# Dealing edge items by TensorE time in a sparse graph network, and writing its tables from ScalarE's queue

## The chip, the core and the metric

The kernel runs on one core of a Trainium2 chip. A core has a matrix engine (TensorE, "PE" in the profile, its weight loads "PEld"), VectorE ("DVE"), ScalarE ("ACT"), GpSimd ("POOL") and a fifth engine that only issues DMAs (SyncE, "SP"). Each engine works through its own queue in order and waits on semaphores for the others; a "q" behind an engine's name (SPq, ACTq) is the queue of that engine, where DMA issues and semaphore waits stand. The metric is device microseconds of one execution.

## The reference

Thirty-two samples of a graph of N = 512 nodes with D = 256 features pass through four layers that share one adjacency matrix `adj` (512 x 512, about 1.8% of its cells nonzero).

```python
def gnn(h, adj, W1, b1, W2, b2, Wa, ba, Wm, bm, beta1, beta2, beta3):   # layers 0 and 3
    pre_u = einsum('bud,dk->buk', h, W1[:D]); pre_v = einsum('bvd,dk->bvk', h, W1[D:])
    hidden = relu(pre_u[:, :, None, :] + pre_v[:, None, :, :] + b1)
    S = sigmoid(einsum('buvk,ko->buvo', hidden, W2)[..., 0] + b2[0])
    a = einsum('buv,bud->bvd', S * adj, h)
    m = einsum('uv,bud->bvd', adj, h) * h
    return beta1 * h + beta2 * (a @ Wa + ba) + beta3 * (m @ Wm + bm)

def layer1(z):  return z + relu(einsum('ij,bjd->bid', adj, z) @ W.T + b)

def layer2(x):
    feats = x @ W1.T
    f1 = feats @ W2 + b2[0]
    coefs = softmax(leaky_relu(f1[:, :, None] + f1[:, None, :]) + adj, axis=-1)
    return coefs @ feats + bias2 + x
```

The gate S is wanted only where `adj` is not zero, since it is multiplied by it.

## The kernel before

**Tiling.** The samples are worked in 8 groups of NB = 4 samples. A sample's 512 nodes lie in NC = 4 chunks of 128 partitions, its 256 features in DC = 2 chunks. A branch at run time takes a path for sparse adjacencies (class `Sparse`); it is the one that runs here, and everything below is of it.

**The edges.** For each group and each of the layers 0 and 3, `pre` (lines 662 to 687) multiplies the turned features by W1: for each sample b and chunk c TensorE's two matmuls (L672, L674) give both halves, VectorE adds the bias to one half while it copies it to the tile `puv` (L677), ScalarE copies the other half (L680), VectorE sums a few mixed columns (L682), and a DMA (L686) writes `puv` (256 KB) to a table in device memory. `puv` has three buffers. The DMA of a piece isn't issued at once: `self.later` holds it, and `settle` issues it, on SP's queue, in the next piece or at the end of a stage.

When a group's table stands, `edges` (L715 on) runs 40 turns, the "edge items". For each of them GpSimd gathers rows of the table by an indirect DMA (L711; the fixed side `mine` is loaded on SP's queue, L766), VectorE takes the maximum, the minimum and a sign product (L805, L807, L806), the row is summed by VectorE (L825) or by ScalarE (L791), and after every few items a sigmoid follows (L749, ScalarE's exponential at L696, L700, L701, L755). The values are scattered by GpSimd (L705) into a dense array of cells, which `load` reads back as the tile `SA`.

**The middle stage.** `middle` and `middle_one` do the rest of layer 0, layers 1 and 2 and the tables of layer 3 for the four samples of a group, as a sequence of pieces (each `yield` ends one). For a sample b they are, in order: `mhT` (two pieces, L49 and VectorE's L874); `pz` (two, L964); `Wm` (two, L971, with VectorE adding to the tile hT, now zT, at L972); `zW` (two, L985, copied by ScalarE at L989); `yT` (two, L49 with `adjT` and zW, ScalarE's L995, VectorE's L996); `feats` (four, L1007, ScalarE's L1015); the softmax (f1 at L1023, and for each of four chunks ScalarE's L1031, VectorE's L1032 and L1034, ScalarE's exponential at L1035, VectorE's L1036 and the scaling L1037; `put_back` turns a finished chunk on TensorE at L1076 and ScalarE copies it at L1077); between the last put_backs the next sample's `hWa` (two, L49 with Wa); the weighted sum `pv` (two, L49 with eT, VectorE's L1054 making xT in the buffer of yT); `flat` for the next sample (ScalarE, L933); `pre` for layer 3 (four); and turning x2 back (two, L1065, ScalarE's copy L1067 and DMA L1068, issued on ScalarE's queue). For group 0, `hWa` and `mhT` have been made ahead (`middle_before`) and aren't in the stage. The last stage of a group (`last`: L49, L1125, L1134) and the first stage of a later one (`first`: turning the input, L658 and L659, then `pre`) are streams of their own.

**The order.** `weave` (L543 on) takes all streams, each with a list of times for its pieces, sorts all pieces by time, and has them emitted in that order. The times only order the pieces; they aren't times on the chip. The middle stages are the "main" streams. A stage's pieces get times in proportion to the shares that `middle_shares` lists: `spread` gives each piece its start, and the next piece starts as much later as the share says. The 40 turns of an edge stream lie at even steps over a stretch of time. So a piece with a large share has more edge items behind it in the queues. For group g's middle stage these are items of layer 0 of the next group and of layer 3 of the group before. Pieces of `first` and `last` ("fill") run only behind a middle piece that yields True (the last one of Wm, zW, yT, feats and pv, and each of the softmax): one of them, or two when four or more are due. The operations of an edge item are kept by `behind` from being scheduled ahead of the middle piece two back.

**Ends.** Before the first middle stage lies a prelude (the lists of edges, group 0's tables and edge items), behind the last one the layer 3 edges and the last stage of group 7.

Of the kernel before, what the change touches and what calls it, by code (L numbers as in the profile page):

```python
# [19 lines left out]
NC = N // P  # L20
DC = D // P
G = 32
NB = 4
# [28 lines left out]
class Model:  # L52


    def __init__(self, ctx, tc, a):
        nc = self.nc = tc.nc
        self.tc, self.a = tc, a
        const = self.const = ctx.enter_context(tc.tile_pool(name="const", bufs=1))

        self.cols = const.tile([P, 2, 2, DC, 1], F32, name="cols_W2_b1")  # L60
        for k, L in enumerate(("L0_gnn", "L3_gnn")):
            nc.gpsimd.dma_start(self.cols[:, k, 0], a[f"{L}_W2"].rearrange("(c p) o -> p c o", p=P))
            nc.gpsimd.dma_start(self.cols[:, k, 1], a[f"{L}_b1"].rearrange("(c p o) -> p c o", p=P, o=1))
        self.ident = const.tile([P, P], F32, name="ident")
        make_identity(nc, self.ident)
        self.adj = const.tile([P, NC, N], F32, name="adj")
        for c in range(NC):
            nc.sync.dma_start(self.adj[:, c, :], a["adj"][c * P : (c + 1) * P, :])
        self.g0, self.g3 = self.gnn_first("L0_gnn"), self.gnn_first("L3_gnn")
# [444 lines left out]
class Sparse:  # L514
# [3 lines left out]
    def __init__(self, ctx, m, counts, xr, outr, B):  # L518
        self.m, self.nc, self.tc, self.counts = m, m.nc, m.tc, counts
        tc = m.tc  # L520
        self.xr, self.outr = xr, outr
        pool = lambda n, b, **k: ctx.enter_context(tc.tile_pool(name=n, bufs=b, **k))
        self.dram = pool("dram", 1, space=bass.MemoryType.DRAM)

        self.cells = {
            k: [self.dram.tile([CELLS + SPARE, NB], F32, name=f"cells_{k}{q}") for q in range(2)] for k in "03"
        }
        self.lists = self.dram.tile([N, 2 * N], F32, name="lists")
        self.x2s = self.dram.tile([B, P, NC, D], F32, name="x2s")

        self.xT, self.x2T = (self.dram.tile([B, P, DC, N], F32, name=n) for n in ("xT", "x2T"))
        self.e = Edges(m, pool("edges", 1))
        self.adjT = pool("adjT1", 1).tile([P, NC, N], F32, name="adjT")
        self.grp = pool("grp", 2)
        self.act, self.small, self.gath = pool("act", 1), pool("small", 2), pool("gath", 6)
        self.ps = pool("ps", 7, space=PSUM)
        self.ps_f1 = pool("ps_f1", 1, space=PSUM)
        self.later, self.bigs, self.given, self.marks = None, 0, None, {}

    def psum(self):  # L540
        return self.ps.tile([P, N], F32, name="pst", tag="pst")
# [120 lines left out]
    def pre(self, g, b, hT):  # L662

        nc, w = self.nc, g.w
        rows = g.table.rearrange("(c p k) (b d) -> p c k b d", p=P, k=2, b=NB)
        for c in range(NC):
            cs = slice(c * P, (c + 1) * P)
            if c % 2 == 0:
                two = [self.psum() for _ in range(2)]
                for k, pp in enumerate(two):  # L670
                    ks = slice((c + k) * P, (c + k + 1) * P)
                    nc.tensor.matmul(pp, hT[:, 0, ks], w["W1"][:, 0::DC, :], start=True, stop=False)  # L672
            pp = two[c % 2]
            nc.tensor.matmul(pp, hT[:, 1, cs], w["W1"][:, 1::DC, :], start=False, stop=True)  # L674
            puv = self.small.tile([P, 2, D], F32, name="puv", bufs=3)
            part, mixed = (g.parts[:, k, c, b : b + 1] for k in range(2))
            nc.vector.scalar_tensor_tensor(  # L677
                puv[:, 0, :], pp[:, 0:D], 1.0, w["bu"], ALU.mult, ALU.add, accum_out=part
            )
            nc.scalar.copy(puv[:, 1, :], pp[:, D:])  # L680
            junk = self.small.tile([P, MIXED.stop - MIXED.start], F32, name="mixed", bufs=1)
            nc.vector.scalar_tensor_tensor(  # L682
                junk, puv[:, 0, MIXED], 1.0, w["sign"][:, 0, :], ALU.mult, ALU.mult, accum_out=mixed
            )
            self.settle()
            self.later = lambda c=c, puv=puv: nc.sync.dma_start(rows[:, c, :, b, :], puv)  # L686
            yield

    def settle(self):

        if self.later:
            self.later()
        self.later = None

    def exp_of(self, w, t):
        self.behind(self.nc.scalar.activation(t, t, AF.Exp, bias=w["nb2"], scale=-1.0))  # L696
# [18 lines left out]
    def edges(self, g, spare=()):  # L715
# [9 lines left out]
        mine = {}  # L725
        places = g.table.rearrange("(c p k) n -> c k p n", p=P, k=2)
        first, mixed, behind = (slice(0, MIXED.stop), MIXED, slice(MIXED.stop, D))
        sign = w["sign"][:, 1, :].unsqueeze(1).to_broadcast([P, NB, MIXED.stop - MIXED.start])

# [149 lines left out]
    def first(self, g, i):  # L879


        def load(b):
            h = self.act.tile([P, NC, D], F32, name="h0", tag="h", bufs=2)
            self.nc.sync.dma_start(h, self.xr[i + b])
            return h

        h = load(0)
        for b in range(NB):
            ahead = load(b + 1) if b < NB - 1 else None
            hT = self.turned(h, "hT0", "hT")  # L890
            yield
            self.nc.scalar.dma_start(self.xT[i + b], hT)
            yield from self.pre(g, b, hT)
            h = ahead
        self.settle()

    def middle_before(self, g0, i):

# [13 lines left out]
    def middle(self, g0, g3, i):  # L912


        SA = self.load(g0, 0)
        given, self.given = self.given, None
        h, hT = self.fresh(i, given)
        hT = hT()
        hWa = None
        if not given:  # L920
            for hWa in self.hWa(g0, hT, 0):
                yield
        flat = self.flat(SA, 0)
        for b in range(NB):
            keep = [h, hT, hWa, flat]
            yield from self.middle_one(g0, g3, b, i + b, SA, keep, given)
            h, hT, hWa, flat = keep
        self.settle()

    def flat(self, SA, b):  # L930
        flat = self.act.tile([P, NC, N], F32, name="flat", tag="eT")
# [255 lines left out]
def middle_shares(given):  # L1187


    hWa = [] if given else [1.7, 1.7]  # L1190
    shares = list(hWa)
    for b in range(NB):
        more = hWa if b < NB - 1 else []
        shares += [] if given else [2.8, 2.8]
        shares += [3.4, 3.4, 1.0, 2.7]
        shares += [1.7, 3.4, 2.8, 4.5] + [0.9] * NC
        shares += [0.4, 0.4, 0.4, 1.0, 0.4, 1.0] + more + [1.5, 1.5]
        shares += [2.8, 4.5] + [0.4] * NC + [0.5, 0.5]
    return shares + [0.1]


# [1 line left out]
def sparse_path(ctx, m, counts, xr, outr, B):  # L1203
# [10 lines left out]
    for t in range(last + 1):  # L1214
# [17 lines left out]
        if t == last:  # L1232
            end -= 0.2
            edges3 = edge_times(end + 0.003, end + 0.02, end + 0.45, end + 0.46, LEAD_AT_ENDS)
            behind = end + 0.29, end + 0.45
        streams += [
            (sp.first(g0, t * NB), first, "fill"),
            (sp.edges(g0, ("yT", "mhT3") if t == 0 else ()), edges0, ""),
            (sp.middle(g0, g3, t * NB), spread(middle_shares(t == 0), start, end), "main"),
            (sp.edges(g3, ("yT", "h1", "hT1") if t == last else ()), edges3, "free"),  # L1240
        ]
# [245 lines left out]
```

## Time and profile before

| | |
|---|---|
| median of 3 runs | 3185.09 us (3176.19, 3185.09, 3185.63) |
| profiled execution | 3185.67 us |
| its span in the profile | 3184.0 us |
| mean granted clock of TensorE | 0.936 |
| busy: PE, DVE, ACT, POOL | 2747.2, 2113.7, 1345.4, 1571.7 us |
| prelude and stage of group 0 | 0 to 264, 264 to 507 us |
| stages of groups 1 to 6 | 507 to 2690 us, about 364 us each |
| stage of group 7, end | 2690 to 2910, 2910 to 3184 us |

A row of the profile's groups names line, engine, operation, output <- input by the program's names, and the number of them; a DMA's row ends with the time from issue to landing. A row of the waits names who waited, for whom, the total in microseconds, how often, and the longest. Where zT is added in the tile hT, it is called hT; xT lies in the tile yT. In group 3 the four samples' stretches are 1230 to 1321, 1321 to 1407.7, 1407.7 to 1503 and 1503 to 1594 us. The granted clock is a share of TensorE's full speed.

### The profile page before, as it was taken

The page shows a single profiled execution, that of the slowest core. Times are in us where ns is not written, and L with a number is a line of the kernel's source. Part 1 is how long each engine was busy: PE and PEld are TensorE (multiplying, and loading weights), DVE is VectorE, ACT ScalarE, POOL GpSimd, SP SyncE. Part 2 cuts the span into 40 slices and gives each one's busy share as a digit, 9 for nine tenths or more (in the row PEclk, how much of TensorE's full clock was granted, in tenths as well). Part 3 has the DMA queues.
Part 4 walks back from the last instruction along what each step waited for, and adds up shares of the span by engine and source line. Part 5 has one row for each costly group of instructions (what it writes and reads, how often), then busy time and mean ns, then how long its engine had stood idle before and what let it go on. Part 6 is the DMA issues. An engine that isn't in the chain of part 4 may idle for free. (4 is left out here: it accounts for less than half of the span.)

```text
span 3184.0 us, 32606 instructions
## 1 busy us (share of the span) xinstructions
PE 2747.2 (86%) x8729; PEld 1664.7 (52%) x8730; DVE 2113.7 (66%) x5600; ACT 1345.4 (42%) x4185; POOL 1571.7 (49%) x1519
## 2 busy tenths in 40 slices
PE   6555888879998899989998899988999799989948
PEld 3333444445664565545654465545654466545637
DVE  6662686667587785777667785777758684773651
ACT  3343554444354343544345343544335343543330
POOL 2462454556455563555445563456535563450460
PEclk9787889999999999999999999999999999989979
DMA  8874557777678766887678766686678766651763
GB/s 282 288 228 152 187 188 228 241 261 221 207 236 261 238 220 220 264 263 227 200 242 265 260 222 213 228 283 217 202 236 263 267 217 219 197 188 66 244 199 113
DMA packets 315329, 712.73 MB, mean 224 GB/s; under 512 B 57600, under 2 KB 175360, under 8 KB 306944
## 3 DMA queue, kind: packets, MB, share of 16 engines
q0 software_dynamic: 133824, 439.85, 42.8%
q1 hardware_dynamic: 162928, 234.01, 22.5%
q10 hardware_dynamic: 18384, 36.71, 3.1%
q8 instruction: 71, 1.16, 0.2%
q14 instruction: 122, 1.00, 0.1%
HBM read 564.28 MB, written 146.15 MB: 223 GB/s over the span
## 5 line engine op out<-in xcount | busy, mean ns | idle before, releaser
L705 POOL DMA_INDIRECT cells<-s,cell x640 | 718.1, 1122 | 774.6 <-DMA cells<-s,cell 571.7
L711 POOL DMA_INDIRECT rows<-table,iv x556 | 598.4, 1076 | 612.1 <-DMA less<-less 235.5
L791 ACT ACTIVATE rows<-rows 128x256 f32<-128x256 f32 x1164 | 470.5, 406 | 620.8 <-DVE rows L807 371.4
L805 DVE TENSOR_TENSOR rows<-rows,mine 128x576 f32<-128x576 f32 x618 | 463.1, 749 | 238.8 <-DMA rows<-table,iv 215.9
L49 PE MATMUL pst<-adj,h 128*128 128x512 f32 x1024 | 452.2, 593 | 0.0
L825 DVE TENSOR_REDUCE s<-rows 128x4 f32<-128x1024 f32 x327 | 396.3, 1212 | 3.1
L49 PE MATMUL pst<-L_gnn_Wa,hT 128*128 128x256 f32 x1024 | 269.6, 415 | 131.8 <-DMA hT<-xT 73.2
L807 DVE TENSOR_TENSOR rows<-rows,mine 128x448 f32<-128x448 f32 x618 | 380.6, 616 | 0.0
L49 PEld LDWEIGHTS pst<-adj,h 128*128 128x128 f32 x1024 | 193.1, 191 | 220.4 <-issue 217.2
L49 PEld LDWEIGHTS pst<-L_gnn_Wa,hT 128*128 128x128 f32 x1024 | 210.6, 211 | 181.8 <-issue 68.0
L677 DVE SCALAR_TENSOR_TENSOR puv<-pst,L_gnn_bu 128x256 f32<-128x256 f32 x256 | 107.0, 418 | 238.5 <-DMA table<-puv 166.1
L49 PE MATMUL pst<-eT,feats 128*128 128x512 f32 x512 | 233.9, 611 | 12.9 <-ACT eT L1077 12.9
L49 PE MATMUL pst<-adjT,zW 128*128 128x512 f32 x512 | 226.3, 595 | 7.5 <-ACT zW L989 7.5
L985 PE MATMUL pst<-WT,hT 128*128 128x256 f32 x512 | 150.9, 460 | 79.6 <-DVE hT L972 79.6
L791 ACT ACTIVATION_READ_ACCUMULATOR rows<-rows 128x1 f32 x1164 | 219.3, 188 | 0.0
L1125 PEld LDWEIGHTS pst<-hWa,SA 128*128 128x128 f32 x896 | 213.7, 327 | 7.7 <-issue 5.0
L1125 PE MATMUL pst<-hWa,SA 128*128 128x256 f32 x896 | 216.8, 398 | 0.0
L933 ACT COPY flat<-SA 128x512 f32<-128x512 f32 x128 | 136.6, 1125 | 186.5 <-DMA SA<-cells 80.4
L680 ACT COPY puv<-pst 128x256 f32<-128x256 f32 x256 | 92.3, 370 | 249.1 <-DVE puv L677 246.2
L964 PE MATMUL pst<-flat,hWa 128*128 128x512 f32 x448 | 196.8, 592 | 0.0
L985 PEld LDWEIGHTS pst<-WT,hT 128*128 128x128 f32 x512 | 118.3, 236 | 118.9 <-DVE hT L972 54.4
L806 DVE TENSOR_TENSOR rows<-rows,L_gnn_sign 128x128 f32<-128x128 f32 x618 | 171.7, 279 | 0.0
(215 smaller groups left out, 4009.9 us busy)
## 6 DMA issues: line engine op xcount, KB each, us to landing
table<-puv SPq DMA_DIRECT2D x256, 256.0 KB, 5.1
SA<-cells POOLq DMA_DIRECT2D x64, 1024.0 KB, 6.2
h<-in_x_dram SPq DMA_DIRECT2D x64, 512.0 KB, 6.0
mine<-table SPq DMA_DIRECT2D x64, 512.0 KB, 6.7
rows<-table POOLq DMA_DIRECT2D x62, 512.0 KB, 6.3
hT<-xT SPq DMA_DIRECT2D x36, 512.0 KB, 5.1
h<-x2s SPq DMA_DIRECT2D x36, 512.0 KB, 4.9
xT<-hT ACTq DMA_DIRECT2D x32, 512.0 KB, 6.9
```

Of the source, the lines that this page charges most:

```text
L49: nc.tensor.matmul(out, lhsT, rhs, start=(n == 0), stop=(n == len(pairs) - 1))
L705: self.nc.gpsimd.indirect_dma_start(out=g.cells[half], out_offset=bass.IndirectOffsetOnAxis(ap=at, axis=0), in_=s, in_offset=None)
L711: self.nc.gpsimd.indirect_dma_start(out=rows, out_offset=None, in_=g.table, in_offset=bass.IndirectOffsetOnAxis(ap=at, axis=0))
L791: self.behind(nc.scalar.activation(part, part, AF.Identity, accum_out=g.s[:, k, b : b + 1]))
L805: self.behind(nc.vector.tensor_tensor(rows[:, :, first], rows[:, :, first], other[:, :, first], ALU.max))
L806: nc.vector.tensor_tensor(rows[:, :, mixed], rows[:, :, mixed], sign, ALU.mult)
L807: self.behind(nc.vector.tensor_tensor(rows[:, :, behind], rows[:, :, behind], other[:, :, behind], ALU.min))
L825: nc.vector.tensor_reduce(g.s[:, k, :], rows, AX.X, ALU.add)
L933: self.nc.scalar.copy(flat[:, r, :], SA[r][:, :, b])
L964: nc.tensor.matmul(pz, hWa[:, r, cs], flat[:, r, :], start=(r == 0), stop=False)
L985: nc.tensor.matmul(pw[:, at], zT[:, d, cs], m.WT_1[:, d, :], start=(d + k == 0), stop=(d * k == 1))
L1125: nc.tensor.matmul(pz[:, k * D : (k + 1) * D], SA[r][:, cs, b], hWa[:, r, :], start=(r + k == 0), stop=False)
```

## The change

Two things are changed. `middle_shares` gives other shares to the same pieces of the middle stage: a sample's sum (with hWa and mhT) goes from 52.0 to 71.2; the softmax's pieces go from 0.4 and 1.0 to 1.5 and 2.5, the pieces behind which fill runs grow by about 1, pre's go from 0.4 to 1.0. The number of pieces and the streams' stretches of time stay, so the stage as a whole has the same items; which of its pieces they stand behind is new. And the DMA that writes `puv` to the table is issued on ScalarE's queue in the piece itself, where it was held back by a piece and issued on SP's queue; `settle` and `later` go. All other instructions stay.

```diff
@@ pre @@
-            self.settle()
-            self.later = lambda c=c, puv=puv: nc.sync.dma_start(rows[:, c, :, b, :], puv)
-            yield
-
-    def settle(self):
-
-        if self.later:
-            self.later()
-        self.later = None
+            nc.scalar.dma_start(rows[:, c, :, b, :], puv)
+            yield
...
@@ first, middle @@
-        self.settle()
...
@@ middle_shares @@
     for b in range(NB):
-        more = hWa if b < NB - 1 else []
+        more = 0.0 if given or b == NB - 1 else 1.7
         shares += [] if given else [2.8, 2.8]
-        shares += [3.4, 3.4, 1.0, 2.7]
-        shares += [1.7, 3.4, 2.8, 4.5] + [0.9] * NC
-        shares += [0.4, 0.4, 0.4, 1.0, 0.4, 1.0] + more + [1.5, 1.5]
-        shares += [2.8, 4.5] + [0.4] * NC + [0.5, 0.5]
+        shares += [3.4, 3.4, 1.0, 3.8]
+        shares += [1.7, 4.5, 2.7, 5.5, 0.9, 0.9, 0.9, 3.7]
+        shares += [1.5, 1.5, 1.5, 2.5, 1.5, 2.5]
+        for _ in range(2):
+            shares += [more] if more else []
+            shares += [2.5]
+        shares += [2.7, 5.5] + [1.0] * NC + [0.8, 0.8]
     return shares + [0.1]
```

More of the change, by code (lines that the diff above doesn't have):

```diff
@@ L537, in __init__ @@
         self.ps_f1 = pool("ps_f1", 1, space=PSUM)
-        self.later, self.bigs, self.given, self.marks = None, 0, None, {}
+        self.bigs, self.given, self.marks = 0, None, {}
     def psum(self):
@@ L927, in middle @@
             h, hT, hWa, flat = keep
-        self.settle()
     def flat(self, SA, b):
```

## The prediction

> **What bounds the kernel now.** I read, in this order, the page's first table, the busy time by stretches, the waits of TensorE, the same waits sample by sample within one group, and the rows of the moved DMA.
>
> ```profile
> PE 2747.2 (86%) x8729; PEld 1664.7 (52%) x8730; DVE 2113.7 (66%) x5600; ACT 1345.4 (42%) x4185; POOL 1571.7 (49%) x1519
> ```
> ```profile
> 0.00:264.00 264.00, 147.33 (x472) 85.96 (x474) 157.30 (x571) 101.22 (x359) 122.42 (x141) 0.83 0.79 263
> 264.00:507.00 243.00, 197.24 (x563) 105.27 (x562) 145.62 (x376) 114.45 (x305) 93.84 (x93) 0.87 0.52 170
> 507.00:2690.00 2183.00, 1992.87 (x6353) 1202.59 (x6352) 1548.95 (x4026) 961.80 (x2974) 1161.83 (x1103) 0.96 0.73 237
> 2690.00:2910.00 220.00, 195.15 (x589) 112.53 (x588) 138.31 (x343) 96.77 (x273) 94.64 (x92) 0.94 0.56 183
> ```
>
> The columns are the stretch, its length, the busy time of PE, PEld, DVE, ACT and POOL, the granted clock, the DMA share and GB/s. Groups 1 to 6 (507 to 2690 us) are two thirds of the span, and TensorE is idle for only 2183.0 - 1992.9 = 190 us of them. No step of the change alters TensorE's work, so what can be won there is this idle time and the clock lost behind it.
>
> ```profile
> PE pst L985 <- DVE hT L972: 73.4, 18, 5.7
> PE pst L1076 <- DVE ex L1037: 42.4, 17, 7.7
> PE pst L1007 <- DVE yT L996: 26.4, 10, 4.5
> PE pst L672 <- ACT hT L659: 13.6, 11, 2.8
> ```
>
> These are TensorE's waits in groups 1 to 6 (total, times, longest). They fall in two places. In the first (L985, L1007) it waits for VectorE to add zT and yT; in the second (L1076) for the softmax's last scaling. VectorE is late there because edge items stand ahead of these operations in its queue. Both places recur in each group at the same samples; in group 3, samples 0, 1 and 2 show
>
> ```profile
> PE pst L985 <- DVE hT L972: 4.6, 1, 4.6
> ...
> PE pst L1076 <- DVE ex L1037: 5.0, 2, 4.6
> PE pst L672 <- ACT hT L659: 2.8, 1, 2.8
> PE pst L985 <- DVE hT L972: 2.2, 1, 2.2
> ...
> PE pst L985 <- DVE hT L972: 5.7, 1, 5.7
> PE pst L1007 <- DVE yT L996: 4.2, 1, 4.2
> PE pst L971 <- DVE mhT L874: 1.5, 1, 1.5
> ```
>
> By the stretches of the four samples TensorE is idle 5.0, 11.2, 12.6 and 0.4 us: 29.2 us a group.
>
> **Part one, the shares.** Before, the softmax of a sample gets little of the 52.0 units of share, so few edge items fall into it; after, it gets more of 71.2. Replaying the order of pieces, the 480 items of 24 samples move so (before, after): mhT and pz 114, 78; Wm and zW 96, 90; yT 72, 60; feats 42, 48; softmax with hWa 84, 138; pv 48, 36; pre and x2 24, 30. One item costs VectorE, from start to start in the timeline, 0.67 + 0.54 + 0.21 us (maximum, minimum, sign), every second one a sum of 1.13 (half: 0.57), and 0.15 for the small ones: 2.14 us.
>
> Before zT. Between one sample's last xT add and the next one's zT add, the built order has 10.9, 24.7, 22.7, 23.3 us of VectorE's work for samples 0 to 3 (its own operations included), and after it 6.9, 19.1, 16.4, 18.4. TensorE's work up to zW is 31.8, 29.2, 26.6, 31.8 us before and 31.8, 28.3, 24.9, 31.8 after. Sample 0's wait of 4.6 loses 4.0 and leaves about 0.7; sample 1's 2.2 goes; sample 2's 5.7 loses 6.3, gets 1.7 back from less cover, and goes to the nearest 1 us. Its next wait, 4.2 for yT, loses 2.4 and gets 1.7 back: 3.5. The 1.5 for mhT goes too. Sum: 18.2 becomes 4.2, won 14.0 a group.
>
> In the softmax. From the feats' column to its last scaling VectorE has 12.2, 11.1, 13.5, 14.2 us before and 14.9, 17.3, 14.5, 19.2 after; from there to the xT add 11.3, 10.6, 10.7, 2.4 and 13.6, 11.9, 15.3, 5.6. TensorE's cover up to the last put_back is 12.5, 11.7, 12.1, 15.6 and 13.4, 13.4, 19.2, 17.4. Sample 0: the first put_back's cover falls from 4.3 to 2.6 us and more stands ahead, so it waits 2.4, and pre waits 1.4 for xT. Sample 1: 6.2 more work less 1.7 more cover on top of 5.0 is 9.5; with the 2.8 (L672) and 0.3 that stay, 12.6. Sample 2: the cover grows by 7.1, no wait. Sample 3: 5.0 more work, less 1.8 cover and 2.3 us by which its scaling was early, is 0.9, and xT 1.1.
>
> A group then idles 4.5 + 12.6 + 3.5 + 2.0 = 22.6 us instead of 29.2: -6.6, and six groups -40 us.
>
> Clock. Behind the 5.66 us wait the matmuls of L985 took 6.61 us:
>
> ```profile
> 1427.29 6.61 PE L985 MATMUL pst<-WT,hT 128*128 128x256 f32 x16 [5.66 <-DVE hT L972]
> ```
> ```profile
> 2913.77 3.45 PE pst L985 x16
> ```
>
> where sixteen without a wait took 3.45 (second line, from the chain that ended last). So a wait of over 3 us costs 3.2 us more. A group has four of them, and by the sum above three: 6 x 3.2 = -19 us. [...]
>
> Group 0 and group 7. Group 0 has no such wait for zT but 24.5 us in four softmaxes (L1076); its softmaxes get 10 items instead of 6, 4 x 2.14 = 8.6, of which I count +7. Group 7 gets 3 more (6.4) and loses about 4 of its 6.2 us at L985: +2.
>
> **Part two, the table writes.** 256 writes move from SP's queue to ScalarE's, each right behind its copy (L680), no longer held back by one piece.
>
> ```profile
> L686 SPq DMA_DIRECT2D table<-puv x256: 512/513/1896, 49.6 to 2964.6; - x128
> ...
> DMA to landing us min/median/max: 2.4/5.1/11.6
> ```
> ```profile
> L1068 ACTq DMA_DIRECT2D x2s<-x x64: 326/327/1292, 333.5 to 2965.4; - x64
> ```
>
> The issue occupies SP's queue 0.513 us (mean 0.566, 145 us in all); ScalarE's own issues of x2 take 0.327, or 84 us for 256. ScalarE then sits between those while flat, the edge sums, feats' copies and the softmax's exponentials queue behind. It is busy 42%, so most of it falls into idle time: at the rate of its busy share in groups 1 to 6 (962 / 2183 = 0.44) 0.44 x 84 = 37 would push something, and about half of what is pushed lies before an operation that TensorE waits for: +20. Ends: nothing and +145. For its data the write adds no wait, since the copy ahead of it waits for the same VectorE operation already (ACT puv L680 <- DVE puv L677, 246 us). But in the built program 122 of the 256 writes also wait for an earlier DMA to land, mostly a load of SP's; the next copies, x2, flat and the edge sums queue behind it. In the middle stages of before these DMAs had landed at least 6.8 us ahead, so I count nothing; without that lead each could cost up to a landing, 5.1 us. The prelude is apart: ScalarE is nearly without idle time from 45 to 91 us there and the first gather comes at 92.2, so 16 writes at 0.33 are +5 (0 to 12).
>
> What SP gains: its writes were issued 0 to 0.4 us behind the copy in most cases, so the landing, and VectorE's 166 us of waits for a free puv (three buffers, 5.1 us to land), stay. Below nothing there is one place: in the prelude hT loads (L944) stand behind L686's waits on SP, and TensorE waits 73.2 us for them; but the first middle stage then waits 12.5 us for flat, which the edge items set, so I count 0 (end: -12). [...]
>
> **Sum.** -40 - 19 + 7 + 2 + 20 + 5 = -25 us. The profiled execution took 3185.67 us (span 3184.0 and 1.7 around it), 0.6 above the median 3185.09; 3185.67 - 25 = 3161.
>
> **The rivals.** What a measurement of this kernel can tell from no change is about 0.3%, 9.6 us.
>
> *VectorE late in the softmax (slower).* The 14.0 us a group won before zT stay. But the extra work up to xT is 5.0, 7.5, 5.6 and 8.2 us, the extra cover 0.9, 1.7, 7.1, 1.8; if samples 0 and 3 have no slack in front of put_back, that is 4.1 + 5.8 + 0 + 6.4 = 16.3 against 14.0, or +2.3 x 6 = +14, and no clock is won. With +9 of groups 0 and 7 and +25 of part two: 3185.67 + 48 = 3234; if one more wait a group passes 3 us, +19: 3253. It decides where the slack there is below some 3 us. For it: the longest such wait is 7.7 us already, in seventeen places. Against: sample 3 has 2.3 us and sample 2 much more cover.
>
> *Gathers even out (much faster).* VectorE waits 215.9 us for gathered rows (L805), in group 3's sample 2 13.2 us in 6 waits; an even deal spaces its requests. If half of the idle in groups 1 to 6 that is left by the forecast (23 x 6 / 2 = 68) goes too: 3161 - 68 = 3093. Against: POOL waits 571.7 us for scatters to land, and the number of gathers under way is the same.
>
> *The waits only move (same).* TensorE reaches the softmax sooner by what it saved before zT and finds VectorE at the same place: part one gives 0 and part two is covered: 3185.
>
> **How the numbers follow.** Forecast 0.40; late softmax 0.36; even gathers 0.11; only moved 0.13. The forecast's own range is 3141 (part two at nothing) to about 3175. The range 3090 to 3245 takes in the fast case and the slower one up to the middle of its additions; left out are part two at +145 (3286) and the upper part of the slower case, under 2 in 10. Faster is the forecast and the even gathers, 0.51, of which 0.01 goes to no change: 0.50; same 0.14; slower 0.36.
>
> **What would show it.** In groups 1 to 6: L985 <- L972 from 73.4 to under 10 us and L1007 <- L996 about 20; L1076 <- L1037 from 42.4 to about 75; TensorE idle from 190 to about 150 us and the clock 0.96 or better. Writes on ScalarE's queue of about 0.33 us, not 0.51. I am wrong if L1076 grows beyond 90 us, if L674 <- L1054 (8.8 us) passes 30, if the writes' rows on ScalarE exceed 0.5 us, or if ScalarE's yT, zW or eT appear as what TensorE waits for.

## The result and the profile after

The changed kernel takes 3236.18 us in the median of four runs (3229.44 to 3238.62), the kernel before 3185.36; the ratio is 1.0163, with a 95% interval from 1.0138 to 1.0187. It is 51 us slower, where 24 us faster was forecast. The profiled execution took 3229.44 us (span 3227.7).

Since the change takes nine lines out ahead of it, a line of the middle stage has a smaller number in the changed kernel: L963 is the L972 of before (zT), L987 is L996 (yT), L1011 is L1020 (the feats' column), L1028 is L1037, L1067 is L1076 (put_back), L1068 is L1077, L924 is L933 (flat), L844 is L851 (loading SA). Among the edge lines, seven lines are out: L798 is L805, L704 is L711.

The first table of the page after (engine, busy us, share, instructions), and then the windows cut where the stages begin and end, first after, then before (columns as above):

```profile
PE 2761.0 (86%) x8729; PEld 1656.0 (51%) x8730; DVE 2119.9 (66%) x5600; ACT 1341.4 (42%) x4185; POOL 1564.8 (48%) x1519
```
```profile
0.00:264.60 264.60, 150.21 (x473) 87.53 (x475) 158.96 (x571) 102.34 (x359) 119.76 (x140) 0.84 0.77 259
264.60:508.60 244.00, 198.30 (x561) 105.23 (x560) 145.32 (x376) 114.35 (x305) 95.31 (x93) 0.86 0.51 170
508.60:2741.50 2232.90, 2008.26 (x6354) 1196.64 (x6353) 1554.87 (x4026) 956.86 (x2974) 1156.96 (x1105) 0.95 0.71 232
2741.50:2947.60 206.10, 182.78 (x574) 105.52 (x573) 136.44 (x342) 96.27 (x272) 98.06 (x92) 0.95 0.60 195
```
```profile
264.50:507.00 242.50, 196.74 (x562) 105.07 (x561) 145.62 (x376) 114.45 (x305) 93.34 (x93) 0.87 0.52 170
507.00:2690.20 2183.20, 1993.07 (x6354) 1202.63 (x6353) 1548.95 (x4026) 961.80 (x2974) 1161.83 (x1103) 0.96 0.73 237
2690.20:2903.30 213.10, 188.25 (x573) 109.45 (x572) 137.62 (x342) 95.95 (x272) 94.64 (x92) 0.94 0.58 189
```

The loss lies wholly in groups 1 to 6: 2232.9 - 2183.2 = +49.7 us (the spans differ by 43.7). The prelude is unchanged (264.6 against 264.5), group 0 takes 1.5 us more and group 7 takes 7.0 us less. In groups 1 to 6 TensorE is idle 224.6 us instead of 190.1, so +34.5, and the other 15.2 is the same matmuls taking longer at a lower granted clock (0.95, before 0.96).

TensorE's waits there, after:

```profile
PE pst L1067 <- DVE ex L1028: 82.9, 21, 9.5
PE pst L49 <- ACT eT L1068: 37.0, 18, 3.4
PE pst L49 <- ACT puv L680: 33.9, 6, 6.4
PE pst L672 <- ACT hT L659: 18.7, 12, 3.2
...
PE pst L998 <- DVE yT L987: 5.7, 6, 1.5
PE pst L976 <- DVE hT L963: 4.6, 7, 1.5
```

The waits for zT (73.4 before) and yT (26.4) are as good as gone. The one in the softmax has doubled (42.4 before; about 75 was forecast), but behind it stand two that the forecast's sum did not contain: the copy into eT (6.7 before), named there only as a sign of being wrong, and puv (7.0). In group 3 the four samples idle 4.9, 16.8, 11.8 and 5.8 us (before: 5.0, 11.2, 12.6, 0.4). TensorE's idle time over all six groups, by sample (each from its first pz to the next one's, in us):

| | sample 0 | 1 | 2 | 3 | all |
|---|---|---|---|---|---|
| before | 40.6 | 72.9 | 69.6 | 7.0 | 190.1 |
| after | 36.9 | 85.2 | 68.6 | 33.9 | 224.6 |
| change | -3.7 | +12.3 | -1.0 | +26.9 | +34.5 |
| change forecast for the shares (six times group 3) | -3.0 | +8.4 | -54.6 | +9.6 | -39.6 |

Samples 2 and 3 of group 3, after:

```profile
PE pst L1067 <- DVE ex L1028: 5.3, 2, 4.7
PE pst L49 <- ACT eT L1068: 3.4, 1, 3.4
```
```profile
PE pst L49 <- ACT puv L680: 5.8, 1, 5.8
```

Sample 2 was to have no wait in the softmax at all. The timeline of VectorE, ScalarE and TensorE shows why it has:

```profile
1464.86 0.76 DVE L798 TENSOR_TENSOR rows<-rows,mine 128x576 f32<-128x576 f32 x1 [11.66 <-DMA rows<-table,iv]
...
1469.16 0.46 DVE L1011 TENSOR_SCALAR fcol<-feats,twob 128x4 f32<-128x4 f32 x1
```
```profile
1469.71 2.42 ACT L1022 ACTIVATE ex<-f,fcol 128x512 f32<-128x512 f32 x4 [14.29 <-DVE fcol L1011]
```
```profile
1474.75 0.70 PE L1067 MATMUL pst<-ident,ex 128*128 128x128 f32 x4 [4.71 <-DVE ex L1028]
```

VectorE stands idle 11.66 us before a gathered row. The feats' column, with which the softmax begins, is queued behind that edge item, so ScalarE waits 14.29 us and the softmax starts some 12 us after its input was ready. GpSimd's timeline has the two loads of SA (1 MB each) right ahead of that gather:

```profile
1453.45 1.18 POOL L844 DMA_DIRECT2D SA<-cells  x2
1454.93 0.99 POOL L704 DMA_INDIRECT rows<-table,iv  x1 [0.30 <-issue]
```

It was issued at 1454.93 and landed 9.9 us later. In the kernel before the same group has such a stall too, 7.66 us, behind a gather with the same two loads ahead of it; but the next thing of the middle stage in VectorE's queue is then yT, and it was part of the 4.2 us that TensorE waited for yT:

```profile
1434.52 1.15 POOL L851 DMA_DIRECT2D SA<-cells  x2 [0.57 <-DMA cells<-s,cell]
1435.97 1.51 POOL L711 DMA_INDIRECT rows<-table,iv  x1 [0.30 <-DVE rows L805]
```
```profile
1447.54 0.76 DVE L805 TENSOR_TENSOR rows<-rows,mine 128x576 f32<-128x576 f32 x1 [7.66 <-DMA rows<-table,iv]
```

It is the same in all six groups: sample 2's longest stall (6.2 to 7.7 us before, 11.7 to 13.1 after) ends with a gather issued right behind two loads of SA, before ahead of yT, after ahead of the feats' column. The items moved, and the stall came to stand in front of another consumer. Before gathered rows VectorE now waits 295.8 us in all (215.9 before).

Sample 3, at the head of ScalarE's queue and on TensorE:

```profile
1603.27 1.09 ACT L924 COPY flat<-SA 128x512 f32<-128x512 f32 x1 [13.31 <-DMA SA<-cells]
1604.27 0.36 ACT L680 COPY puv<-pst 128x256 f32<-128x256 f32 x1
```
```profile
1604.69 3.78 PE L49 MATMUL pst<-L_gnn_Wa,hT 128*128 128x256 f32 x8 [5.76 <-ACT puv L680]
```

The next group's flat waits 13.31 us for its SA; the copies into puv stand behind it in ScalarE's queue, so the tiles `pst` that they read are not freed, and TensorE waits for those. The last two loads of SA were issued at 1598.1, 10.5 us behind pv's end (1587.6); before, they were issued at 1574.3, with pv's end. More edge items of the next group had been put into the last softmax, and so their scatters came later: GpSimd's rows have ten of them from 1569 to 1595, where before the last one was issued at 1571.8.

The writes themselves, on ScalarE's queue:

```profile
L685 ACTq DMA_DIRECT2D table<-puv x256: 520/521/1427, 49.9 to 3007.9; - x128
L685 ACTq EVENT_SEMAPHORE  x122: 17/17/17, 49.5 to 2817.3; - x122
```

An issue takes 0.521 us in the median (forecast: 0.327), with a mean of 0.542, or 139 us in all (the expectations below reckon with 256 x 0.521 = 133); the 122 waits for earlier DMAs never waited (17 ns each).

### The profile page after: what moved, and what is told of

Same layout as the page of the kernel before. It is cut to its first block, busy times and chain, and to the rows that moved or that the text cites. A ratio compares the mean times of both kernels' runs of the same rounds, so it can differ in the third digit from the quotient of the medians.

```text
span 3227.7 us, 32484 instructions
## 1 busy us (share of the span) xinstructions
PE 2761.0 (86%) x8729; PEld 1656.0 (51%) x8730; DVE 2119.9 (66%) x5600; ACT 1341.4 (42%) x4185; POOL 1564.8 (48%) x1519
## 5 line engine op out<-in xcount | busy, mean ns | idle before, releaser
L698 POOL DMA_INDIRECT cells<-s,cell x640 | 717.4, 1121 | 865.8 <-DMA cells<-s,cell 568.0
L704 POOL DMA_INDIRECT rows<-table,iv x556 | 588.7, 1059 | 417.8 <-issue 104.2
L798 DVE TENSOR_TENSOR rows<-rows,mine 128x576 f32<-128x576 f32 x618 | 463.6, 750 | 325.3 <-DMA rows<-table,iv 295.8
L49 PEld LDWEIGHTS pst<-adj,h 128*128 128x128 f32 x1024 | 194.1, 192 | 218.4 <-issue 214.3
L49 PE MATMUL pst<-eT,feats 128*128 128x512 f32 x512 | 262.2, 671 | 42.2 <-ACT eT L1068 42.2
L49 PE MATMUL pst<-adjT,zW 128*128 128x512 f32 x512 | 234.7, 613 | 12.5 <-ACT zW L980 12.4
L924 ACT COPY flat<-SA 128x512 f32<-128x512 f32 x128 | 137.3, 1122 | 255.0 <-PE pst L49 132.0
L1067 PE MATMUL pst<-ident,ex 128*128 128x128 f32 x512 | 93.2, 317 | 140.0 <-DVE ex L1028 102.6
L49 PEld LDWEIGHTS pst<-eT,feats 128*128 128x128 f32 x512 | 107.8, 215 | 183.2 <-issue 128.5
L808 POOL DMA_INDIRECT less<-less,inode x64 | 70.3, 1098 | 219.3 <-DMA less<-less 154.5
```

Of the source, the lines that this page charges most:

```text
L49: nc.tensor.matmul(out, lhsT, rhs, start=(n == 0), stop=(n == len(pairs) - 1))
L698: self.nc.gpsimd.indirect_dma_start(out=g.cells[half], out_offset=bass.IndirectOffsetOnAxis(ap=at, axis=0), in_=s, in_offset=None)
L704: self.nc.gpsimd.indirect_dma_start(out=rows, out_offset=None, in_=g.table, in_offset=bass.IndirectOffsetOnAxis(ap=at, axis=0))
L798: self.behind(nc.vector.tensor_tensor(rows[:, :, first], rows[:, :, first], other[:, :, first], ALU.max))
L924: self.nc.scalar.copy(flat[:, r, :], SA[r][:, :, b])
```

## The experiments

Theory S: the shares are slower by themselves, through the softmax, the displaced gather stall and the late SA. Theory Q: the shares gain as forecast, and it is ScalarE's occupied queue that loses. Runs 1 to 8 and 12 to 15 were on one chip, 9 to 11 on another, each set (1 to 4, 5 to 8, 9 to 11, 12 to 15) beside the kernel before. Its medians there were 3197.9, 3194.3, 3208.2 and 3198.5 us, against 3185.4 beside the changed kernel, so times are compared as ratios. Only the first set has a trace of the kernel before, so waits of later runs are held against a trace from another set; differences of a few microseconds there mean nothing.

**1. The shares alone.** The new `middle_shares` in the kernel before; the writes as before.

```diff
-        shares += [0.4, 0.4, 0.4, 1.0, 0.4, 1.0] + more + [1.5, 1.5]
+        shares += [1.5, 1.5, 1.5, 2.5, 1.5, 2.5]
...
```

> The new shares alone; the table writes stay on SP's queue, held back by a piece. Theory S (the shares explain the slowdown: softmax late in sample 1, a gather stall ahead of the feats' column in sample 2, a late load of SA in sample 3): about 3230, 45 us above before, with the waits of the put_back near 100 us in all. Theory Q (ScalarE, held up by issuing the writes, explains it): no slower than before, 3140 to 3185, and the waits of TensorE for ScalarE (eT, zW, puv) back at before's 13, 8 and 10 us.

Measured: 1.0087 (1.0052 to 1.0122), 28 us slower. Theory Q is out as the sole cause: without any write on ScalarE the waits are

```profile
PE pst L1076 <- DVE ex L1037: 81.1, 30, 10.1
...
PE pst L49 <- ACT eT L1077: 39.3, 25, 3.4
PE pst L49 <- ACT puv L680: 37.2, 7, 9.0
```

in the whole run, where the changed kernel has 102.6, 42.2 and 33.9 and the kernel before 54.8, 12.9 and 8.3. By sample TensorE idles 30.3, 103.1, 55.0 and 35.9 us in the six groups, 224.3 in all: as much as with both parts. But the shares make only half of the loss in time.

**2. The queue alone.**

```diff
-            self.settle()
-            self.later = lambda c=c, puv=puv: nc.sync.dma_start(rows[:, c, :, b, :], puv)
+            nc.scalar.dma_start(rows[:, c, :, b, :], puv)
```

> The writes on ScalarE's queue alone, with the old shares. Theory S: within 10 us of before (3185). Theory Q: 3205 to 3235, with TensorE's waits for eT, zW and puv up by 60 us in all. [...]

Measured: 1.0106 (1.0067 to 1.0145), 34 us slower. Theory S is out as the sole cause too. The waits for eT, zW and puv, which I had named, grew by 4 us in all and not by 60; those for zT and the softmax grew:

```profile
PE pst L976 <- DVE hT L963: 109.1, 21, 12.6
PE pst L1067 <- DVE ex L1028: 88.2, 30, 9.6
```

(79.6 and 54.8 in the whole run before.) An issue is short beside its DMA, 0.521 us against 5.4 us from issue to landing in the changed kernel; on a queue that VectorE and TensorE depend on, the 139 us of issues still cost 34.

Alone, the two parts cost 0.87% and 1.06%, together 1.63%: the sum of both, 1.9%, is a little more, which the intervals don't rule out.

**3. The softmax's old shares in the changed kernel.**

```diff
-        shares += [1.5, 1.5, 1.5, 2.5, 1.5, 2.5]
+        shares += [0.4, 0.4, 0.4, 1.0, 0.4, 1.0]
...
-            shares += [2.5]
+            shares += [1.5]
```

> The changed kernel, but the softmax's pieces keep the old shares (0.4, 0.4, 0.4, 1.0, 0.4, 1.0, 1.5, 1.5): by the replayed order of pieces 78 edge items fall into the softmaxes of 24 samples instead of 138 (before: 84), 60 into pz (after 42, before 72). If items in the softmax are the cause: the put_back waits fall back to about 55 us and the time to 3165 to 3190. If it is the gather stall and the late SA load, whatever the softmax's share: still above 3215.

Measured: 1.0016 (0.9994 to 1.0038). The softmax's share carries most of the loss. (The share of the last feats piece, which the change raises by 2.8 and not by about 1, stays raised here.) ScalarE's waits for the feats' column, 91.5 us in the changed kernel and 1.9 before, are 6.0. What is left is not the forecast gain, though: waits of L998 for yT are 51.5 us in the whole run (28.0 before), those for puv still 28.6.

**4. A gain before zT without the softmax's loss.** The kernel before with mhT 2.0, pz 2.4, yT 3.4 and 5.1, pv 3.4 and 5.1, pre 0.7.

```diff
-        shares += [] if given else [2.8, 2.8]
-        shares += [3.4, 3.4, 1.0, 2.7]
+        shares += [] if given else [2.0, 2.0]
+        shares += [2.4, 2.4, 1.0, 2.7]
...
```

> The kernel before with smaller shares for mhT (2.0) and pz (2.4) and larger ones for yT (3.4, 5.1), pv (3.4, 5.1) and pre (0.7); softmax and queue as before. By the replayed order mhT and pz get 78 items instead of 114, as in the changed kernel, but the softmax 90 instead of 138. If the gain before zT is real and is only outweighed in the softmax: the waits of L985 fall from 80 to under 20 us and the time to 3100 to 3150. If every shift of items merely moves a wait: 3175 to 3195 or slower.

Measured: 0.9991 (0.9972 to 1.001): no difference. The waits for zT fell from 79.6 to 38.0 us (under 20 were expected), and in their place TensorE waits 46.9 for the feats' copies (L1023, 1.3 before) and 36.0 for xT (L674, 8.8 before). The items were dealt elsewhere and the waits followed.

**5. The writes on ScalarE's queue, but held back by a piece as before.**

```diff
-            self.later = lambda c=c, puv=puv: nc.sync.dma_start(rows[:, c, :, b, :], puv)
+            self.later = lambda c=c, puv=puv: nc.scalar.dma_start(rows[:, c, :, b, :], puv)
```

> The kernel before, old shares, its writes still held back by a piece, but issued on ScalarE's queue. If the time that ScalarE's queue is occupied (256 x 0.52 us) is what the second part costs: about 1% slower than before, as with the writes on ScalarE at once (1.06%). If it was the earlier place of the write: within 0.3% of before.

Measured: 1.0124 (1.0092 to 1.0156), as with the writes at once. It is the engine that counts, not the piece.

**6. ScalarE's copy made twice, the writes on SP.**

```diff
             nc.scalar.copy(puv[:, 1, :], pp[:, D:])
+            nc.scalar.copy(puv[:, 1, :], pp[:, D:])
```

> The kernel before, old shares, writes on SP's queue, but ScalarE makes its copy into puv twice: 256 x 0.37 = 94 us more on ScalarE's queue, no DMA moved. If the second part costs by ScalarE's occupied queue (133 us gave 34): 94 / 133 x 34 = +24 us, 0.75%. If it costs by the queue of the DMA, by landing times or by the new order of gathers: within 0.3% of before.

Measured: 1.0079 (1.005 to 1.0108), against 1.0075 expected. With no DMA moved, 95 us more on ScalarE's queue cost 25, about as much for a microsecond as the writes (34 for 139). The largest wait is the same, for zT, but it is only a little above the 79.6 us of before:

```profile
PE pst L986 <- DVE hT L973: 89.7, 22, 9.7
```

So occupied time on ScalarE's queue is enough to explain the second part. One thing stays open: when the program is built, both edits also put VectorE's and GpSimd's instructions in another order (in the traces some 330 of VectorE's 5600 and 110 of GpSimd's 1500 stand elsewhere with the writes moved, 160 and 60 with the second copy). What of the cost is the delay itself and what the new order, these runs don't separate.

**7. The changed kernel with the next group's layer 0 edge items ending earlier.**

```diff
-            edges0 = edge_times(start - 0.552, start - 0.505, start - 0.06, start - 0.04)
+            edges0 = edge_times(start - 0.552, start - 0.505, start - 0.10, start - 0.08)
```

> The changed kernel with the next group's layer 0 edge items ending earlier (start - 0.10 and - 0.08 in place of - 0.06 and - 0.04). If TensorE's 5 to 6 us at the end of each group (behind ScalarE's copies of puv) come from SA's late load, which ScalarE's flat waits for at the head of its queue: that wait falls under 2 us and the time by 6 x 5 = 30 us or a little more. If they come from the writes on ScalarE's queue: it stays, and the time with it.

Measured: 1.0104 (1.0071 to 1.0138), where the changed kernel had 1.0163: 19 us, not 30. The waits behind puv are gone: ScalarE's flat waits 58.6 us for SA instead of 123.0, and sample 3 idles 0.0 us in each of groups 1 to 6. So the late SA is where sample 3's wait came from. But the wait was not won: over the six groups sample 3 idles 33.9 us less and sample 2 idles 32.8 more (101.4 in place of 68.6), largely before f1:

```profile
PE f L1014 <- ACT feats L1006: 44.8, 6, 8.5
```

**8. SA loaded through SP's queue in the changed kernel.**

```diff
-            self.nc.gpsimd.dma_start(t.rearrange("p v b -> p (v b)"), cells.rearrange("(p v) b -> p (v b)", p=P))
+            self.nc.sync.dma_start(t.rearrange("p v b -> p (v b)"), cells.rearrange("(p v) b -> p (v b)", p=P))
```

> The changed kernel with the loads of SA (1 MB each) issued on SP's queue, not GpSimd's. In sample 2 of a group VectorE stands 11.7 us before a gathered row whose gather was issued behind two such loads. If it is the order in that queue: the stall and TensorE's 5.3 + 3.4 us behind it in sample 2 fall by half or more, 6 x 5 = 30 us in all, unless SP's loads of hT and h are held up behind SA's wait for the scatters. If the DMA engines are simply taken by 2 MB: no change.

Measured: 1.0244 (1.0207 to 1.028), slower still. In sample 2 of group 3 the softmax's 5.3 us are gone and the 3.4 for eT shrink to 1.3, but 4.8 us for yT and 2.5 for xT come instead (8.8 idle in all, 11.8 in the changed kernel); and SP's loads of hT stand behind SA's waits for the scatters: TensorE waits 13.5 us for one of them in group 7. The gather with sample 2's longest stall, no longer behind loads of SA, lands in 4.4 us and not in 9.9, and the stall is

```profile
1446.98 0.76 DVE L798 TENSOR_TENSOR rows<-rows,mine 128x576 f32<-128x576 f32 x1 [5.76 <-DMA rows<-table,iv]
```

ahead of yT again. So by this run the loads of SA ahead of the gather are what makes the stall in sample 2 long; moving them to SP's queue is no remedy. What the run doesn't separate is how they hold the gather up: in the changed kernel the DMA share was 0.95 to 1.01 from 1454 to 1465 us, that is, the DMA engines were full, and on SP's queue the loads were issued at 1453.4, 11 us behind the gather. So it may be GpSimd's queue or the full DMA engines.

**9. As 3, with the writes on SP.** The new shares but for the softmax's, in the kernel before.

> The new shares except the softmax's, which stay as before (0.4 to 1.5), with the writes on SP's queue, held back by a piece as before. With the writes on ScalarE's queue these shares gave 1.0016 of before, and those writes alone 1.0106. If the two parts add: 0.991 of before (about -29 us) and faster than both kernels; what the changed kernel lost by its shares is then the softmax's alone. If they do not add (the shares are neutral whatever the queue): within 0.3% of before.

Measured: 0.9995 (0.997 to 1.002). The parts do not add: with these shares the queue makes 0.2% (1.0016 against 0.9995, within their intervals), with the old ones 1.06%. And this is the cleanest test of the forecast's first step: the gain before zT is there, without the softmax's items and without writes on ScalarE. TensorE's waits in groups 1 to 6:

```profile
PE pst L1007 <- DVE yT L996: 59.4, 13, 8.8
PE pst L1076 <- DVE ex L1037: 34.8, 8, 6.2
PE pst L49 <- ACT puv L680: 30.5, 6, 7.1
PE pst L672 <- ACT hT L659: 23.2, 11, 4.5
PE pst L985 <- DVE hT L972: 17.5, 13, 3.4
```

Against the trace of before (of another set): zT 73.4 down to 17.5 and the softmax 42.4 down to 34.8, 64 us won; yT 26.4 up to 59.4, puv 7.0 up to 30.5, hT of L672 13.6 up to 23.2, 66 us lost, and eT and mhT add 15. Nothing of the gain is left, though the softmaxes of 24 samples hold 78 items and not 138. Against run 1 (1.0087), which differs by the softmax's shares alone, their cost is 0.9%.

**10. As 9, edge items ending 0.02 earlier.**

```diff
+            edges0 = edge_times(start - 0.552, start - 0.505, start - 0.08, start - 0.06)
```

> As the one before it, and the next group's layer 0 edge items end 0.02 earlier (start - 0.08, - 0.06). If the wait at the head of ScalarE's queue for SA (flat) also costs here: sample 3's waits behind puv (3 to 6 us a group with the writes on ScalarE's queue) go and the time falls another 10 to 30 us. If the items moved forward meet other waits: the same or slower.

Measured: 0.9987 (0.9962 to 1.0012). The 10 to 30 us did not come: the difference to run 9 is 0.0008, inside both intervals.

**11. The kernel before, edge items ending 0.04 earlier** (the edit of 7).

> The kernel before with the next group's layer 0 edge items ending 0.04 earlier (start - 0.10, - 0.08). Before, TensorE stands 0.4 to 1.9 us a group behind puv in sample 3, so there is little to win: if an earlier end is good by itself, 5 to 15 us faster; if it only pays where SA is late, as in the changed kernel (1.63% there against 1.04% with it): within 0.3% or slower, since the same items are dealt more densely before.

Measured: 0.9935 (0.9905 to 0.9965), faster by 21 us, more than expected: the earlier end pays in the kernel before too, and as much as in the changed one. ScalarE's flat waits 40.7 us for SA (80.4 before), VectorE 107.8 for a free puv (166.1). TensorE's idle time in groups 1 to 6 isn't smaller (196.9 us; 190.1 before, on another chip), so what the gain comes from is not shown.

**12 to 14. Five gathers ahead in place of four**, in the changed kernel, in the kernel before, and in that of run 11.

```diff
-LEAD = 4
+LEAD = 5
```

> The changed kernel with five gathers ahead of the item in work in place of four (LEAD). If VectorE's stalls before gathered rows (296 us in all, 11.7 us in sample 2 ahead of the feats' column) come of too few gathers under way: they fall by a third or more, TensorE's waits in sample 2 (5.3 and 3.4 us) with them, and the time to 1.005 to 1.010 of before. If the gathers are held in GpSimd's queue behind scatters that wait for one another: an earlier place in the order helps little, within 10 us of the changed kernel's 1.0163.

> The kernel before with five gathers ahead. Its stalls before gathered rows are 216 us, of which 7.7 and 1.4 us stand ahead of sample 2's yT and zT. If too few gathers are under way: 10 to 30 us faster (0.99 to 0.997). If the queue is the limit: within 0.3%.

> The kernel before with the layer 0 edge items ending 0.04 earlier and five gathers ahead. The first alone gave 0.9935. If the two causes are separate: the product of both ratios; if they are one (gathers and scatters that share GpSimd's queue): no better than 0.993.

Measured: 1.0211 (1.0171 to 1.0252), 1.0037 (1.001 to 1.0064), 0.9912 (0.9879 to 0.9945). More gathers under way shorten neither kernel by themselves; if anything, both are slower with them (the changed one had 1.0163, and the intervals overlap). VectorE's stalls stay (302.9 and 214.3 us), and GpSimd waits longer for scatters to land in the changed kernel (637.6 us, 568.0 without). So the number of gathers under way is not what limits here. Together with the earlier end it made the fastest kernel of the study; its lead over run 11 is within their intervals.

**15. The shares alone, edge items ending 0.04 earlier.**

> The new shares alone, writes on SP's queue, with the layer 0 edge items ending 0.04 earlier. The shares alone gave 1.0087, and the same step took the changed kernel from 1.0163 to 1.0104. If the late load of SA is part of what the shares cost: 0.6% less, 1.002 to 1.004, and sample 3's 5 us behind puv gone. If it costs only together with writes on ScalarE's queue: still 1.007 or more.

Measured: 1.0044 (1.0026 to 1.0063), against 1.0087 without, near what was expected, and with no write on ScalarE involved. Over the six groups sample 3 idles 0.5 us in place of 35.9, and sample 2 97.5 in place of 55.0; the sum is nearly the same (221.1, 224.3). In group 2 sample 2's 16.7 us lie mostly before f1 and for xT.

This does not make the late SA half of what the shares cost, since run 11 shows that the same step takes 0.65% off the kernel before. With the early end on both sides the shares cost 1.0044 / 0.9935 = 1.011 (1.0087 without it), and the whole change 1.0104 / 0.9935 = 1.017 (1.0163). The early end is a gain of its own; that the late SA is a part of the loss is not shown.

## Why the prediction was wrong

The profiled execution was forecast to become 25 us shorter and became 43.7 longer. Of these 69 us, 55 are idle time in groups 1 to 6 (forecast -40 by the shares and +20 by the writes, +34.5 measured) and 34 are the clock there (-19, +15.2); the smaller terms were 20 us too high. By run 1, the shares alone were forecast at -50 us and cost 28. The step that failed is the sum of idle time in the softmax, in sample 2 above all: over the six groups that sample was to idle 55 us less. It idles 1 us less (15 by run 1), because the sum held the work in VectorE's queue and not VectorE's own wait for a gathered row.

**Before zT: right at its place, wrong as a gain.** Forecast for groups 1 to 6 were waits for zT under 10 us and for yT about 20; they are 4.6 and 5.7. But runs 4 and 9 show the gain given back at once: the step assumed that a wait removed is time won. VectorE's stall before gathered rows in sample 2 and the late SA in sample 3 come from GpSimd's gathers and scatters and the loads; depending on how the items are dealt, they fall in front of zT, yT, f1, the softmax or puv, and TensorE waits there instead.

**In the softmax: samples 0 and 1 nearly right, 2 and 3 wrong.** In group 3, sample 0: 2.4 us forecast for put_back and 1.4 behind it (for xT), 2.4 and 2.4 (for eT) measured. Sample 1: 9.5 forecast and 9.5 measured; 2.8 us for zW come on top. Sample 2 was given no wait in the softmax because its cover grew by 7.1 us; it has 5.3 and 3.4. The sum counted the work in VectorE's queue and not its idle time, 11.66 us before one gather, though the profile of before had the 13.2 us of sample 2's stalls in it, and I used them only as a rival. Sample 3: 2.0 forecast, 5.8 measured, from the late SA: the sum looked at items only as VectorE's work, and never asked when their scatters would end. Idle in group 3: 22.6 forecast, 39.2 measured; in the mean of the six groups 37.4 (31.7 before, so group 3 with its 29.2 was a little better than the mean).

**Clock.** Forecast -19 us, for one wait of over 3 us a group fewer. The price of 3.2 us came from one row, behind a wait of 5.66 us; no row was given for the limit of 3 us. Groups 1 to 6 have 27 such waits after as before, and TensorE's busy time there grew by 15.2. The limit did not hold either. In the clock's records before, 27 of the 28 stretches at half speed (a granted clock of 0.5) go with such a wait (the other with one of 2.96 us), 164 us in all; at half speed half of it is lost, 3.0 us a wait, close to the price of 3.2. After there are 39 stretches, 205 us in all, and 14 of them go with waits of 1.9 to 2.8 us, which the sum took for free, while two waits of 3.4 us have none. The same matmuls without a wait (granted clock 1.00 from 1580 to 1588 us) and behind one of 2.42 us (0.81 from 1303.6 to 1312.5), both after:

```profile
1580.70 7.03 PE L49 MATMUL pst<-eT,feats 128*128 128x512 f32 x16
```
```profile
1303.68 8.83 PE L49 MATMUL pst<-eT,feats 128*128 128x512 f32 x16 [2.42 <-ACT eT L1068]
```

The prediction's limit of 3 us does not cover a wait of 2.42 us; why the clock falls there is not shown.

**Groups 0 and 7, prelude.** +7, +2 and +5 forecast; +1.5, -7.0 and +0.1 measured. All three were too high, by 19 us together, which made the miss smaller: luck.

**ScalarE's queue.** +25 forecast for both places, 34 (21 to 46) measured alone: about right in size. The issue was priced by the wrong row, 0.327 us where L686's own row had 0.513; with the 139 us measured the same working gives 0.44 x 139 / 2 = 31. That half of what is pushed matters was a guess that no run tests. Run 6 shows that occupied time on ScalarE's queue is enough; through which of its instructions (flat, the edge sums, copies) it reaches zT and the softmax is not shown. The queued waits for earlier DMAs cost nothing, as counted.

**The signs of being wrong.** Two of the four came: the writes' rows exceed 0.5 us, and eT appears among TensorE's waits (37.0 us). L1076 stayed under 90 us (82.9) and xT's wait under 30 (13.9).

**The rivals.** The measured 3236 is within 2 us of the rival in which VectorE is late in the softmax (3234), and runs 3 and 9 show that the softmax's share is what separates the changed kernel from no loss. Yet that the number fits is luck: the rival's sum (no slack in samples 0 and 3, none lost in sample 2) is not what happened; in group 3 sample 3 has no wait in put_back, and sample 2 has one. "The waits only move" is what runs 4 and 9 show for the shares outside the softmax. "Gathers even out" is refuted: the stalls grew by 80 us.

## What to carry to other kernels

Where the engine that waits and the one that it waits for are both busy most of the time (here 86% and 66%), a wait that is removed is not yet time won: ask what the engine waits for next, and whether an idle stretch of the *producer* (here VectorE's before a gather), which no sum of queued work contains, will merely fall in front of another consumer. Look at a stall's cause on the queue where it arises: six times the longest stall of a sample came behind the same two loads. Moving work later in a stage also moves the end of its chain: the items' scatters, the load behind them and whatever stands behind that load's first reader in its engine's queue (here the last loads of SA came 10.5 us behind pv's end, flat waited 13.31 us for them, and TensorE 5.76 behind it). An issue of half a microsecond on an engine that computes is work of that engine (here 0.521 us, 256 times, for 34 us of the kernel's time); price it by a row of the queue that it leaves, not by the cheapest issue on the queue that it joins.

## What the runs showed that was not expected

A second copy of 0.37 us on an engine that is 42% busy cost a quarter of its time (25 of 95 us), and an issue of 0.52 us about the same share (34 of 139). Ending the next group's edge items earlier by 0.04 of a stage is worth 0.65% to the kernel before, 0.6% to the changed one and 0.4% to the shares alone. TensorE's granted clock fell to 0.5 behind waits of 1.9 to 2.8 us (14 of 39 stretches in groups 1 to 6 after) and not only behind longer ones. The kernel before took 3185 to 3208 us in the median from one set of runs to another, a spread of 0.7%, so profiles of two sets can't be held against each other to a few microseconds.
